# A first batch centred by an estimate of its mean and repaired afterwards, and a bias moved from ScalarE into VectorE's sum

## The chip, the cores and the metric

The kernel runs on one core of one Trainium2 chip. TensorE is called PE in the profile, VectorE DVE, ScalarE ACT, GpSimd POOL and SyncE SP. The metric is the device time of one execution in microseconds (us), and what counts is the median of several. The profile is of one further execution; its span runs from that execution's first to its last instruction.

## The reference

The input is x, 4 images of 48 channels and 256 x 256 pixels in float32. Four layers follow each other, each of the form x = x + layer(groupnorm(x)), the group norm having 16 groups of 3 channels without weights.

```python
def _L0_conv_ref(x, qkv_w, dw_w, proj_w, temperature):
    qkv = conv1x1(x, qkv_w)                      # 48 -> 144 channels
    qkv = depthwise3x3(qkv, dw_w)                # padding 1
    q, k, v = split(qkv, 3)                      # each 48 x 65536 per image
    q, k = l2_normalize(q), l2_normalize(k)      # along the pixels
    attn = softmax(q @ k.T * temperature)        # 48 x 48 per image
    return conv1x1(attn @ v, proj_w)

def _L1_conv_ref(x, W1, b1, gamma, beta, dw_w, dw_b, pw_w, pw_b, W2, b2):
    t = gelu(gelu(tokens(x) @ W1 + b1))          # 16 features
    x1, x2 = halves(t)
    n = layernorm(x2, gamma, beta)               # image of 8 channels
    g = x1 * ((depthwise3x3(n) + dw_b) * (conv1x1(n) + pw_b))
    return g @ W2 + b2
```

Layers 2 and 3 are recurrences over rows and columns (a five-tap convolution over channels, added line by line, down, up, right and left). The change doesn't touch them.

## The kernel before

**Layer 0, the sums over pixels (`layers01`, lines 122 to 624).** The attention matrix of an image needs only the products of q and k summed over all pixels, and these follow from "lag sums" of the input: for each shift of up to two pixels the 48 x 48 sums of x at a pixel times x at the shifted pixel. The input x has its group mean taken off first, so that a pixel outside the image counts as zero. For each image b (a batch here) nine pairs of pixel rows are loaded (`load_pair`, line 334; `raw`, 1728 KB each, four buffers), centred in place (`center`, line 341; three instructions a pair, with the means of `means_of`, line 307, which are spread to the rows by six matmuls into `pmask`) and turned into sums and differences (`points`, line 350; six DVE instructions, tiles `moving` and `still`, two buffers each). There are 16 units of work in a batch, two for each of eight pairs of neighbouring row pairs; unit u is 96 matmul calls (192 instructions) into three PSUM tiles `acc` (`sums`, line 367). After unit 15 the tiles are kept, combined to lags (`lags_of`, line 383) and turned into weights of the layer's convolution (`attention`, line 422); this runs in small pieces (`late`) between the next batch's matmuls.

**The statistics.** The mean of batch b + 1 is found while batch b is summed: 16 tiles of 96 x 2048 (`input_stats`, line 182, two loads of 384 KB a tile; called "I tiles" here), the first read by four `bn_stats` of DVE, the rest by two passes of ACT (`rough`, line 155, one writing a scrap tile `seen`, one in place). For batch 0 this stands ahead of the loop: lines 243 to 250 load 12 tiles of 128 x 2048 (`first_stats`, 1024 KB each, "F tiles"), four `bn_stats` each, and `first_norm` makes the mean and the coefficients of batch 0. Only then come the constants and the tap weights (lines 253 to 283), and the loop at line 590. All tiles of statistics share the pool `sums_p` with two buffers; of the F tiles before, every other one borrows a buffer of `moving`.

**Layer 0's convolution and layer 1.** From about 850 us the convolution runs block by block (`block`, line 679; a block makes 16 rows of one image, tile `y`, PSUM `py`). Of its 64 blocks those of image 0 run alone, the others between the pieces of layer 1 (`gated_layer`, line 781; `tick`, line 1067). A tick takes one of 32 strips through: tokens transposed (`ptok`), two projections with gelu (`ph`), a layer norm (`pm`, `pvar`, a reciprocal), convolutions (`psp`, `pch`), gate `g`, and with two ticks' delay the output: matmuls into `pout`, to which DVE adds the strip of x, `xr` (line 1027, 16 instructions of 96 x 256 a tick), after ACT has added the bias b2 to `xr` in place (`add_b2`, line 997, two passes of 96 x 2048 a tick). POOL then rearranges the result (`yr`, line 1034). While convolution blocks remain, `conv` pieces stand between the pieces of a tick; the last ticks have none left (`alone`).

**What sets the order.** Each engine and each DMA queue runs its instructions in the order of the built program. The framework that builds it decides that order from the order of the calls, its tiles and its own estimates; `tc.keep_in_program_order` pins single instructions. The order in the changed program, where the prediction speaks of it, was read from the built program. SP issues nearly all loads and stores, one after the other; an entry that waits for a buffer holds up all that follow.

Of the kernel before, what the change touches and what calls it, by code (L numbers as in the profile page):

```python
# [18 lines left out]
P = 96  # L19
# [102 lines left out]
def layers01(ctx, tc, x, xp, xe, inside, pick, rows, xc, x1, wqk, dwqk, wv, dwv, projT, temp, k, coef, coef1, gated, spare):  # L122
# [30 lines left out]
    seen = work.tile([P, n_st], F32, tag="seen", name="seen", bufs=1)  # L153

    def rough(b, i, t):
# [10 lines left out]
        for s, func in enumerate((AF.Identity, AF.Square)):  # L166
            kept = t if s else seen
            nc.scalar.activation(kept, t, func, bias=away, accum_out=sums[:, s, i - 1 : i])
# [28 lines left out]
    rows_sb = wp.tile([128, KR * (P + 128)], F32, tag="rows", name="rows_sb")  # L197
    nc.scalar.dma_start(rows_sb, rows)
    to_group = lambda m: rows_sb[:, P * m : P * m + P]
    to_row = lambda m: rows_sb[:P, KR * P + 128 * m : KR * P + 128 * m + 128]  # L200
    stat0 = work.tile([128, KR, 4 * NS, 6], F32, tag="st0_0", name="st0_0", bufs=1)
    x0 = x[0:C].rearrange("c (e n) -> (c e) n", e=8)

    def first_stats(i):
        m, part = divmod(i, NS)
        if i % 2:
            t = sums_p.tile([128, n_st], F32, tag="sx", name="sx")
        else:
            t = patch.tile([128, NPT * (PW // 2 + 4) * C], F32, tag="moving", name="sx")[:, :n_st]
        nc.sync.dma_start(t, x0[128 * m : 128 * m + 128, part * n_st : part * n_st + n_st])  # L210

        def add():
            for c in range(4):
                nc.vector.bn_stats(stat0[:, m, part * 4 + c, :], t[:, c * 512 : (c + 1) * 512])

        return add

    def first_norm():

        mv = work.tile([128, KR, 2], F32, tag="mv00", name="mv00", bufs=1)  # L220
        for m in range(KR):
            nc.vector.bn_aggr(mv[:, m], stat0[:, m].rearrange("p a b -> p (a b)"))

        def average(src, name):
            ps = p_small.tile([P, 1], F32, tag="small", name=name)
            for m in range(KR):
                nc.tensor.matmul(ps, lhsT=to_group(m), rhs=src(m), start=m == 0, stop=m == KR - 1)
            return ps

        nc.vector.tensor_copy(mean[0], average(lambda m: mv[:, m, 0:1], "pg"))  # L230
        ps = p_small.tile([128, KR], F32, tag="small", name="prows")
        for m in range(KR):
            nc.tensor.matmul(ps[:, m : m + 1], lhsT=to_row(m), rhs=mean[0], start=True, stop=True)
        d = work.tile([128, KR], F32, tag="d00", name="d00", bufs=1)
        nc.vector.tensor_sub(d, mv[:, :, 0], ps)
        nc.vector.tensor_mul(d, d, d)
        nc.vector.tensor_add(d, d, mv[:, :, 1])
        s = work.tile([P, 1], F32, tag="s00", name="s00", bufs=1)
        nc.scalar.activation(s, average(lambda m: d[:, m : m + 1], "pv"), AF.Sqrt, bias=k.eps[:P])
        nc.vector.reciprocal(coef[0][:, 0:1], s)  # L240
        nc.vector.scalar_tensor_tensor(coef[0][:, 1:2], mean[0], -1.0, coef[0][:, 0:1], ALU.mult, ALU.mult)

    waiting = []
    for i in range(KR * NS):
        waiting.append(first_stats(i))
        if len(waiting) > 3:
            waiting.pop(0)()
    for add in waiting:
        add()
    first_norm()  # L250


    wqk_sb = wp.tile([P, P], F32, tag="wqk", name="wqk_sb")
    nc.sync.dma_start(wqk_sb, wqk)
    wd = wp.tile([P, 3, 3, P], F32, tag="wd", name="wd")
    nc.gpsimd.dma_start(wd.rearrange("p x y o -> p (x y o)"), dwqk.rearrange("t o -> (t o)").partition_broadcast(P))
    for t in range(9):
        nc.vector.tensor_mul(wd[:, t // 3, t % 3, :], wd[:, t // 3, t % 3, :], wqk_sb)

    inside_sb = wp.tile([C, 6 * 128], F32, tag="inside", name="inside_sb")  # L260
    nc.sync.dma_start(inside_sb, inside)
    pick_sb = wp.tile([128, 3, 3, C], F32, tag="pick", name="pick_sb")
    nc.sync.dma_start(pick_sb.rearrange("p d k c -> p (d k c)"), pick)

    w0 = wp.tile([P, 3, 3, P], F32, tag="w0", name="w0")
    w1 = wp.tile([P, 3, 3, P], F32, tag="w1", name="w1")

    wc = wp.tile([P, 2, 2, P], F32, tag="wc", name="wc")
    for i in range(3):
        nc.vector.tensor_scalar_mul(w0[:, i], wd[:, i], half[:, 0:1])  # L270
        nc.vector.tensor_scalar_mul(w1[:, i], wd[:, i], half[:, 1:2])
    for side, tx in enumerate((2, 0)):
        nc.vector.tensor_add(wc[:, side, 0], w0[:, tx, 1], w1[:, tx, 2])
        nc.vector.tensor_add(wc[:, side, 1], w0[:, tx, 0], w1[:, tx, 1])

    wv_sb = wp.tile([C, 2 * 128], F32, tag="wv", name="wv_sb")
    nc.sync.dma_start(wv_sb, wv)
    dwv_sb = wp.tile([C, 9], F32, tag="dwv", name="dwv_sb")
    nc.sync.dma_start(dwv_sb, dwv)
    proj_sb = wp.tile([C, C], F32, tag="proj", name="proj_sb")  # L280
    nc.sync.dma_start(proj_sb, projT)
    temp_sb = wp.tile([C, 1], F32, tag="temp", name="temp_sb")
    nc.gpsimd.dma_start(temp_sb, temp.partition_broadcast(C))


# [21 lines left out]
    def means_of(b):  # L307

        dm = work.tile([C, C], F32, tag="dm", name="dm")
        nc.vector.tensor_scalar(dm, k["ident", C][:, :C], mean[b][:C], -1.0, ALU.mult, ALU.mult)  # L310
# [23 lines left out]
    def load_pair():  # L334

        b, r = pairs[len(raws)]
        t = patch.tile([128, 2, HALO * C], F32, tag="raw", name="raw", bufs=AHEAD + 1)
        nc.sync.dma_start(t, rows_of(xp[b], PH + 2)[:, 2 * r : 2 * r + 2])
        raws.append(t)

    def center(b, r, means):
# [3 lines left out]
        for i, w0, w1 in ((0, 1, PW // 2 + 1), (1, 0, 1), (2, PW // 2 + 1, HALO // 2)):  # L345
            here = wide[:, :, w0:w1]
            mean = means[:, v + i : v + i + 1].unsqueeze(1).to_broadcast([128, 2, w1 - w0, 2 * C])
            nc.vector.tensor_add(here, here, mean)

    def points(b, q, half):  # L350
# [6 lines left out]
        nc.vector.tensor_sub(bt[:, 0], d[0], d[2])  # L357
        nc.vector.tensor_add(bt[:, 1], d[1], d[2])
        nc.vector.tensor_add(at[:, 0], r[0], r[1])
        nc.vector.tensor_sub(bt[:, 2], d[2], d[1])  # L360
        nc.vector.tensor_sub(at[:, 1], r[0], r[1])  # L361
        nc.vector.tensor_sub(bt[:, 3], d[1], d[3])
# [20 lines left out]
    def lags_of(acc):  # L383
# [14 lines left out]
        def combined(d):  # L398
            ways = ((0, 0), (1, 0), (2, 0), (2, 1))
            out = held["out"] = p_small.tile([C, 5, C], F32, tag="small", name="plag")  # L400
            for n, (k, at) in enumerate(ways):
# [5 lines left out]
                    stop=n == len(ways) - 1,  # L407
# [177 lines left out]
    load_pair()  # L585
    load_pair()
    means[0] = means_of(0)
    for r in range(2):
        center(0, r, means[0])
    for g in range(B * NU + 1):  # L590
        b, u = divmod(g, NU)
        if g < B * NU:
            q, part = divmod(u, 2)
            if u == 0:
                of_batch[b] = (weights_of(b), *edges_of(b))
            if part == 0:
                while len(raws) < min(len(pairs), b * (N2 + 1) + q + AHEAD + 1):
                    load_pair()
                if q + 2 <= N2:
                    center(b, q + 2, means[b])  # L600
            new = points(b, q, part)
            if u == NU - 1 and b + 1 < B:
                means[b + 1] = means_of(b + 1)
# [7 lines left out]
        if g > 0:  # L611
# [6 lines left out]
            if u == NU - 1:  # L618
                while late:
                    some_late()  # L620
                first, lags = lags_of(acc)
# [159 lines left out]
def gated_layer(ctx, tc, banks, p_small, big, spare, x1, x2r, w1, w2, dw, ends, pw, cols, b2, k, coef1, coef2):  # L781
# [215 lines left out]
    def add_b2(c, ip):  # L997
        t = xrs[c, ip]
# [787 lines left out]
```

## Time and profile before

| | |
|---|---|
| median of 3 runs | 6943.6 us (6930.9 to 6946.0) |
| the profiled execution | 6936.42 us |
| its span | 6934.4 us |
| mean granted TensorE clock | 0.973 |
| busy: PE / DVE / ACT / POOL | 6569.4 / 3636.3 / 1844.0 / 2069.2 us |
| `acc` matmuls (L374), two forms | 685.6 and 682.5 us |
| sum of pout and xr (L1027) | 512 instructions, 176.7 us |
| bias of xr (L999) | 64 instructions, 127.5 us |
| statistics of batch 0 (L214) | 48 instructions, 28.9 us |

The page gives the busy time of each engine, the span in 40 slices (one is 173 us) with the busy share in tenths, the chain of work that ended last, and the costliest groups of instructions. A line of a timeline has the start in us, the time from the first to the last of a run of equal instructions, engine, line, operation, output <- inputs, shapes, the count, and in brackets the idle time before it with what ended it. A line of the waits has who waited for whom, the total in us, how many times and the longest. PE's busy time hides how fast it runs, and a wait on an engine that isn't the bottleneck costs nothing.

### The profile page before, as it was taken

The numbers are of one execution on the slowest core, as the hardware profiler recorded it, in microseconds if no ns is written. First come the engines' busy times: TensorE is split into PE (matmuls) and PEld (weight loads), VectorE is DVE, ScalarE is ACT, GpSimd is POOL, SyncE is SP. The second block draws the span as 40 slices with busy tenths as digits, with TensorE's granted clock in tenths as the row PEclk, the third lists the DMA queues.
The fourth block names the chain that finished last, engine by engine and source line by source line (L and its number), as shares of the span: only waits on it lengthen the run. The fifth ranks groups of instructions, "written<-read, shape, count | busy, mean of one in ns | idle before, by whom it ended". The sixth has DMA issues, their size and how long they took to land.

```text
span 6934.4 us, 133567 instructions
## 1 busy us (share of the span) xinstructions
PE 6569.4 (95%) x55772; PEld 5266.6 (76%) x55772; DVE 3636.3 (52%) x8740; ACT 1844.0 (27%) x2166; POOL 2069.2 (30%) x4211
## 2 busy tenths in 40 slices
PE   6999999999999779999998999986899999999999
PEld 4666633333333229999998999986899999999999
DVE  7777533555556554444444446754444444444444
ACT  3430022444444434444440000001544443000000
POOL 0000000233333554420004557652000000555777
PEclk9999999999999879999999999998999999999999
DMA  7742145677777769984669678989995566865775
GB/s 237 185 136 84 61 133 176 165 199 195 196 199 184 158 148 301 287 245 155 187 179 226 195 172 205 248 243 188 182 183 95 170 195 171 235 186 168 276 300 201
DMA packets 1177469, 1326.21 MB, mean 191 GB/s; under 512 B 831040, under 2 KB 1005760, under 8 KB 1124512
## 3 DMA queue, kind: packets, MB, share of 16 engines
q1 hardware_dynamic: 1163696, 1229.16, 65.4%
q10 hardware_dynamic: 13072, 88.18, 3.7%
q8 instruction: 437, 7.16, 0.4%
q14 instruction: 168, 1.38, 0.1%
q0 software_dynamic: 96, 0.33, 0.0%
HBM read 794.28 MB, written 522.19 MB: 190 GB/s over the span
## 4 chain that ended last, share of the span: by engine, by line
PE 86%; DVE 4%; DMA 3%; SPq 2%; ACT 2%; POOL 1%; issue 1%; ACTq 0%; POOLq 0%; DVEq 0%
PE ps L1227 57%; PE py L701 9%; PE acc L374 8%; PE py L710 5%; SPq L1263 2%; PE ph L830 2%; PE pout L1018 1%; PE psp L975 1%; DMA D<-d 1%; ACT d L1302 1%; POOL s L1512 1%; PE ptok L890 1%; DVE y L724 0%; DVE st L726 0%; DVE y L1027 0%
## 5 line engine op out<-in xcount | busy, mean ns | idle before, releaser
L1227 PE MATMUL ps<-d,w 128*128 128x128 f32 (+1 forms) x18360 | 2073.8, 276 | 104.3 <-DVE d L1233 61.1
L1227 PEld LDWEIGHTS ps<-d,w 128*128 128x128 f32 x18360 | 2069.2, 193 | 108.8 <-DVE d L1233 64.7
L1227 PE MATMUL ps<-r,w 128*128 128x128 f32 (+1 forms) x18360 | 2066.7, 276 | 68.7 <-POOL r L1444 36.0
L1227 PEld LDWEIGHTS ps<-r,w 128*128 128x128 f32 x18360 | 2064.6, 193 | 70.9 <-POOL r L1444 37.0
L1233 DVE SCALAR_TENSOR_TENSOR d<-ps,b,d 128x128 f32<-128x128 f32 x3054 | 979.7, 348 | 1155.4 <-PE ps L1227 1077.2
L1512 POOL TENSOR_TENSOR s<-s,r 128x128 f32<-128x128 f32 x1536 | 745.4, 521 | 334.3 <-DVE r L1233 331.0
L1233 DVE SCALAR_TENSOR_TENSOR r<-ps,b,pre 128x128 f32<-128x128 f32 x1530 | 490.3, 348 | 577.1 <-PE ps L1227 569.0
L1233 DVE SCALAR_TENSOR_TENSOR r<-ps,b,r 128x128 f32<-128x128 f32 x1530 | 490.1, 348 | 459.1 <-PE ps L1227 431.4
L374 PE MATMUL acc<-moving,raw 128*32 128x240 f32 (+1 forms) x6144 | 685.6, 381 | 12.3 <-DVE moving L357 11.5
L1444 POOL COPY pre<-c 128x128 f32<-128x128 f32 x1530 | 558.4, 404 | 464.3 <-DVE r L1233 462.5
L701 PE MATMUL py<-x1n,wy 128*96 128x512 f32 x1536 | 691.6, 599 | 0.0
L374 PE MATMUL acc<-moving,still 128*32 128x240 f32 (+1 forms) x6144 | 682.5, 381 | 6.8 <-DVE still L361 2.7
L1302 ACT ACTIVATE d<-x,spread 128x256 f32<-128x256 f32 x752 | 510.9, 824 | 550.2 <-DMA D<-d 380.6
L1383 ACT COPY u<-d 128x384 f32<-128x384 f32 x510 | 448.5, 900 | 573.5 <-DVE d L1233 541.0
L374 PEld LDWEIGHTS acc<-moving,raw 128*32 128x32 f32 x6144 | 430.0, 110 | 213.6 <-DVE moving L357 11.8
L701 PEld LDWEIGHTS py<-x1n,wy 128*96 128x96 f32 x1536 | 242.0, 163 | 410.8 <-issue 376.3
L1444 POOL COPY r<-c 128x128 f32<-128x128 f32 x6 | 2.4, 393 | 1691.2 <-DMA c<-U 1691.2
L724 DVE TENSOR_TENSOR y<-py,t 96x512 f32<-96x512 f32 x256 | 173.6, 678 | 462.1 <-PE py L710 462.0
L374 PEld LDWEIGHTS acc<-moving,still 128*32 128x32 f32 x6144 | 345.0, 110 | 34.7 <-issue 4.6
L710 PE MATMUL py<-x2n,wy 64*96 64x512 f32 x1536 | 360.8, 601 | 0.0
L1034 POOL COPY yr<-y 96x256 f32<-96x256 f32 x512 | 307.2, 648 | 129.4 <-DVE y L1027 128.4
L654 ACT ACTIVATE x1n<-t,g 128x2048 f32<-128x2048 f32 x64 | 134.2, 2096 | 696.1 <-PE py L701 573.9
(219 smaller groups left out, 4076.2 us busy)
## 6 DMA issues: line engine op xcount, KB each, us to landing
t<-in_xc SPq DMA_DIRECT2D x64, 1536.0 KB
c<-U SPq DMA_DIRECT2D x348, 256.0 KB
D<-d SPq DMA_DIRECT2D x54, 1536.0 KB
d<-D SPq DMA_DIRECT2D x54, 1536.0 KB
R<-r SPq DMA_DIRECT2D x54, 1536.0 KB
r<-R ACTq DMA_DIRECT2D x54, 1536.0 KB
U<-u SPq DMA_DIRECT2D x84, 768.0 KB
raw<-in_xp SPq DMA_DIRECT2D x36, 1728.0 KB
```

What stands on the lines that cost most here:

```text
L374: nc.tensor.matmul(out[32 * i : 32 * i + 32, : n * C], lhsT=still[i][:, first : first + 32], rhs=moving[:, i, lo : lo + n * C], start=u == ...
L701: nc.tensor.matmul(ps, lhsT=held["w"][0][:, dx], rhs=x1n[:, 2 * c : 2 * c + 2, dx : dx + W], start=dx == 0, stop=False)
L710: nc.tensor.matmul(held["ps"][q + 2 * s], lhsT=held["w"][1][here, dx], rhs=x2n[here, 2 * q : 2 * q + 2, dx : dx + W], start=False, stop=dx ...
L724: nc.vector.tensor_add(part, held["ps"][c], t1[:P, 2 * c : 2 * c + 2, :])
L830: nc.tensor.matmul(out[32 * q : 32 * q + 32], lhsT=w1_sb[:, half, i, :], rhs=moving(t), start=i < 4, stop=i >= 4)
L1034: made = nc.gpsimd.tensor_copy(yrs[c][:, :, 2 * i2 + ip, :].rearrange("p j (n a g) -> p j n a g", a=4, g=4)[:, :, :, al], y[:, i2, al].rea ...
L1227: nc.tensor.matmul(ps[m][:, here], lhsT=w[:, n, :], rhs=old[:, q, there], start=first, stop=last)
L1233: nc.vector.scalar_tensor_tensor(new[:, m], ps[m], bias[:, m : m + 1], inp[:, m], ALU.add, ALU.add)
L1302: pin(nc.scalar.activation(dst, src, AF.Identity, bias=g[:, 1:2], scale=g[:, 0:1]))
L1383: nc.scalar.copy(v[:, :, i, :, al], line)
L1444: nc.gpsimd.tensor_copy(dst[:, m].rearrange("p (J a b) -> p J a b", J=NBK, b=B), v[:, m, j, :, gl].rearrange("p J b a -> p J a b"),)
L1512: nc.gpsimd.tensor_add(v, v, line[:, m].rearrange("p (J a b) -> p J a b", J=NBK, b=B))
```

## The change

**Part 1.** Batch 0 is centred by an estimate of its mean, made ahead of its statistics. The host lays out the image's frame, the outer two pixels on every side (2032 pixels), as `xf` (128 x 768). `guessed` sums it and divides by 2048. The pixel pairs of batch 0 are centred with this estimate; the first two pairs are loaded and centred in two parts, the first halves of both ahead of the rest. The F tiles are now read during batch 0, one in most units, all from the pool `sums_p`; `first_norm`, cut into pieces, runs at the end of batch 0. As the estimate is off by a constant per channel, the lag sums of batch 0 get a repair: sums over the pixels that a shift moves out of the image (they all lie in the frame, `poff`: 20 matmuls), and one more matmul for each of three lag rows (`fixl`, `fixr`). These terms are sums over the true mean and the estimate, so that the lags come out as with the true mean. The weights and edges of batch 0 are made after its last unit. The constants move to ACT's and POOL's queues, behind the first halves; the taps are made after unit 2's points. On the way, DVE's instructions up to unit 2 are pinned, and `rough` drops the scrap tile: the second pass of ACT reads what the first wrote.

**Part 2.** `add_b2` goes; the bias is added in DVE's sum of `pout` and `xr`.

```diff
-        for s, func in enumerate((AF.Identity, AF.Square)):
-            kept = t if s else seen
-            nc.scalar.activation(kept, t, func, bias=away, accum_out=sums[:, s, i - 1 : i])
+        nc.scalar.activation(t, t, AF.Identity, bias=away, accum_out=sums[:, 0, i - 1 : i])
+        nc.scalar.activation(t, t, AF.Square, accum_out=sums[:, 1, i - 1 : i])
...
+    xf_sb = wp.tile([128, NF, C], F32, tag="xf", name="xf_sb")
+    nc.scalar.dma_start(xf_sb.rearrange("p k c -> p (k c)"), xf)
...
-        if i % 2:
-            t = sums_p.tile([128, n_st], F32, tag="sx", name="sx")
-        else:
-            t = patch.tile([128, NPT * (PW // 2 + 4) * C], F32, tag="moving", name="sx")[:, :n_st]
+        t = sums_p.tile([128, n_st], F32, tag="sx", name="sx")
...
+    def guessed():
+        part = work.tile([128, C], F32, tag="gpart", name="gpart", bufs=1)
+        nc.vector.reduce_sum(part, xf_sb.rearrange("p k c -> p c k"), axis=AX.X)
+        ps = p_small.tile([P, 1], F32, tag="small", name="pguess")
+        nc.tensor.matmul(ps[:C], lhsT=part, rhs=k["ones", 128][:, 0:1], start=True, stop=True)
+        nc.vector.tensor_scalar_mul(guess[:C], ps[:C], 1.0 / (128 * NF))
...
+        def outside():
+            ps = held["ps"] = p_small.tile([48, 2, C], F32, tag="small", name="poff")
+            for i in range(NF):
+                nc.tensor.matmul(ps[:, 0], lhsT=off(i), rhs=xf_sb[:, i], start=i == 0, stop=False)
+            for i in range(3):
+                nc.tensor.matmul(ps[:, 0], lhsT=fixed(i), rhs=dg[:, i], start=False, stop=i == 2)
+            nc.tensor.matmul(ps[:, 1], lhsT=k["ones", C][:, :48], rhs=dg[:, 2], start=True, stop=True)
+
+        def factors():
...
+            nc.vector.tensor_mul(
+                right, at.unsqueeze(1).to_broadcast([48, NL, C]), which.unsqueeze(2).to_broadcast([48, NL, C])
+            )
...
-    waiting = []
-    for i in range(KR * NS):
-        waiting.append(first_stats(i))
-        if len(waiting) > 3:
-            waiting.pop(0)()
-    for add in waiting:
-        add()
-    first_norm()
...
+            if b == 0:
+                nc.tensor.matmul(
+                    out.rearrange("p l c -> p (l c)"),
+                    lhsT=fix["left"],
+                    rhs=fix["right"][:, 5 * d : 5 * d + 5].rearrange("p l c -> p (l c)"),
+                    start=False,
+                    stop=True,
                 )
...
-    load_pair()
-    load_pair()
-    means[0] = means_of(0)
+    load_pair(None, 0, FIRST)
+    load_pair(None, 0, FIRST)
+    load_part(0, FIRST, HALO * C, raws[1][:1, 1, FIRST - 1 : FIRST])
+    load_part(1, FIRST, HALO * C)
+    for _ in range(2):
+        load_pair(raws[1][:1, 1, HALO * C - 1 : HALO * C])
+    load_fixed(raws[1][:1, 1, FIRST - 1 : FIRST])
+    guessed()
+    means[0] = means_of(guess)
     for r in range(2):
-        center(0, r, means[0])
+        center(0, r, means[0], 0)
+    firsts = list(range(KR * NS))
...
-                if q + 2 <= N2:
+                if g > 0 and q + 2 <= N2:
                     center(b, q + 2, means[b])
+            if g == 1:
+                for r in range(2):
+                    center(0, r, means[0], 1)
             new = points(b, q, part)
+            if g == 1:
+                center(0, 2, means[0])
+            if g == 2:
+                make_taps()
+                early.clear()
+            if b == 0:
+                for n in range(len(firsts) - KR * NS * max(fed - 1 - u, 0) // fed):
+                    while len(adding) > 1:
+                        adding.pop(0)()
+                    adding.append(first_stats(firsts.pop(0)))
+                if u == fed:
+                    while adding:
+                        adding.pop(0)()
+                    for piece in first_norm():
+                        late.append(piece)
...
-                first, lags = lags_of(acc)
+                if b == 0:
+                    of_batch[0] = (weights_of(0), *edges_of(0))
+                first, lags = lags_of(b, acc)
...
-    def add_b2(c, ip):
-        t = xrs[c, ip]
-        nc.scalar.activation(t, t, AF.Identity, bias=b2_sb)
-
...
-                nc.vector.tensor_add(y[:, q % 2, 2 * kk + q // 2, :], ps[q][:, kk], t[:, 4 * kk + q, :])
+                nc.vector.scalar_tensor_tensor(
+                    y[:, q % 2, 2 * kk + q // 2, :], ps[q][:, kk], b2_sb, t[:, 4 * kk + q, :], ALU.add, ALU.add
+                )
...
-            pieces += [conv] + turned(0, 1) + of_now(centered) + turned(3) + of_old(gate) + added
+            pieces += [conv] + turned(0, 1) + of_now(centered) + turned(3) + of_old(gate)
```

The one-element copies of POOL in `load_part` and `load_fixed` write into the tile that is loaded next, reading the end of one that must have landed; the load then waits for them, which sets the order of the loads.

## The prediction

> **What bounds the kernel now.** I read the page first: the slices of its second part and the chain of its fourth.
>
> ```profile
> span 6934.4 us, 133567 instructions
> PE   6999999999999779999998999986899999999999
> ...
> PE 86%; DVE 4%; DMA 3%; SPq 2%; ACT 2%; POOL 1%; issue 1%; ACTq 0%; POOLq 0%; DVEq 0%
> ```
>
> PE is the bound nearly everywhere. Two places stand out: the first slice (6) and slices 14 and 15 (77). The change touches just these two, so everything between counts only if it breaks PE's cover.
>
> Then the timeline of the first 72 us, for the first place.
>
> ```profile
> 11.44 9.80 DVE L214 BATCH_NORM_STATS2 st<-sx 128x6 f32<-128x512 f32 x16 [11.44 <-DMA sx<-in_x]
> ...
> 49.85 2.76 PE L313 MATMUL pmask<-dm,inside_sb 48*128 48x48 f32 x12 [3.52 <-ACT ends L304]
> ...
> 53.57 3.90 DVE L348 TENSOR_TENSOR raw<-raw,means 128x3072 f32<-128x3072 f32 x3
> ...
> 64.13 1.01 PE L374 MATMUL acc<-moving,raw 128*32 128x240 f32 x2 [11.52 <-DVE moving L357]
> ...
> 71.01 1.15 DVE L357 TENSOR_TENSOR moving<-raw 128x960 f32<-128x960 f32 x1
> ```
>
> The reader sees 48 statistics instructions (16 in 9.8 us, so 2.45 us a tile of four), then the norm, the centring, and only at 64.13 the first product; the points of unit 0 are complete at 71.1. From there PE sets the pace: the loads of raw pairs, each waiting for PE, are issued at 92.08, 112.80, 133.52, 154.24 and 174.96, so two units take 20.72 and one 10.36 us. Batch 0 ends at 245.4, where ACT's copy of acc stops waiting.
>
> For the second place I read the waits between 2240 and 2640 us, where the last images run without convolutions between them.
>
> ```profile
> DVE y L1027 <- ACT xr L999: 23.5, 7, 5.8
> ```
>
> Seven times DVE's sum waited for ACT's bias. The timelines of ACT and DVE show one turn:
>
> ```profile
> 2424.93 1.29 ACT L946 ACTIVATE n<-d,col 128x512 f32<-128x512 f32 x1 [4.22 <-DVE d L944]
> 2426.02 1.96 ACT L999 ACTIVATE xr<-xr,b_sb 96x2048 f32<-96x2048 f32 x1
> ```
> ```profile
> 2428.01 2.74 DVE L1027 TENSOR_TENSOR y<-pout,xr 96x256 f32<-96x256 f32 x8 [3.11 <-ACT xr L999]
> ```
>
> PE's next matmul (ph, 2428.91) waits for that y.
>
> **Part 1, the start.** Removed ahead of the first product: twelve F tiles (first batch's statistics, 1 MB each), the norm and the taps. Put there: xf, 0.39 MB, at the place in ACT's queue where rows_sb (0.34 MB) was, whose last packet ended at 5.2 us in the trace; I take 6.2. Then the sum over 768 elements 0.9 (a 768-column still takes 0.95), its matmul and copy 0.8, dm 0.25, the pmask row 2.8, three copies 1.06: means at 12.1. The two first halves land in the place of the first F tiles (first read at 11.44). Centring them is 1920 of 3456 columns of a 3.81 us pitch each, 4.3 together: 16.4. First moving: **17.5**; points take 6.02 a unit (243.53 to 249.54 in DVE's timeline), so unit 0's are complete at 22.4. That is 48.7 us earlier. The sum over xf reads with a stride and has no row of its own, no more than the repair's broadcast product later (48x720): I take the plain rows of their size (0.95, and 0.8 for 720 columns), and as the dear end 3.35, the reciprocal of 512 columns, the slowest DVE row of that size. Bounds of the first product: 17 (centring right at 11.44) and 24 (xf served only with the second F tile, whose last packet ended at 12.9).
>
> **What takes its place in batch 0.** The rest of the loads moves behind the first halves: the second halves, the fixed tensors (1.5 MB, now on ACT's and POOL's queues) and raws 2 and 3 are 5.8 MB, from 13.8 to 28.6 at 390 GB/s (380 was the rate of 40 to 60 us), so F0 is there at 32. POOL's one-element copies order them: 0.1 us like its memsets, up to 0.65 like its smallest copies; nothing waits for them, as centre 2 begins at 31.9.
>
> DVE per two units: 12.0 points, 3.8 centring, 1.71 F tiles at 2.45: 20.0 of PE's 20.72. It fits, but with no room, and the order on DVE is fixed: in the changed program it runs points 0, rest of the centring, points 1, centre 2, F0, I0 (I: next batch's tiles), F1, centre 3, points 2, taps and F2, points 3. Step by step: points 1 end 31.9, centre 2 35.7, F0 and I0 with their few small sums 41.0. F1 may be loaded only when F0's buffer is read (38.2); 1 MB takes 2.5 us (419 GB/s in the DMA view while F tiles came alone), start and landing 2.1: DVE idles to 42.8. Then F1 45.3, centre 3 49.1, points 2 55.1. PE, which began unit 1 at 33 (a unit ends some 10.6 us after its points when PE was idle), is done with it at 43.3 and gets unit 2 only now: **11 us lost**. Taps (4.9) and F2 make points 3 end at 68.5, unit 3 three late; by unit 6 the sum of losses is 16, and the one turn where a centring and an F tile stand inside the points (unit 10) adds 1.5. From then PE is the bound. 22.4 + 10.6 + 15 x 10.36 + 17.5: batch 0 ends at **206**, for 245.4.
>
> The loads: raw, I and F tiles need 4.4 to 4.9, 3.45 and 2.5 us of the DMA engines, 17.1 per 20.72 us, so they fit. SP's queue is in order, and the tiles alternate between two buffers, so nearly all I tiles follow each other in one. A turn of it is landing plus two passes of ACT (4.2):
>
> ```profile
> 92.08 0.35 SPq L338 DMA_DIRECT2D raw<-in_xp  x1
> 92.54 16.85 SPq L186 DMA_DIRECT2D sx<-in_x  x6
> ```
> ```profile
> 104.36 2.00 ACT L168 ACTIVATE seen<-sx,away 96x2048 f32<-96x2048 f32 x1 [6.87 <-DMA sx<-in_x]
> ```
>
> Behind a raw the turn is 11.8 + 4.2 = 16.0; alone it was 9.9 (free at 108.5, landed 114.4). Stepping through SP's order gives the last I tile done at 198, 12.1 a turn over 13 turns from 41. PE asks for it at 81% of unit 15, about 203: it is hidden, by 5 to 8 us.
>
> **The turn of the batches.** Before, the next batch's norm stood in unit 14, and its two pairs were centred (7.7 us) beside unit 15. In the changed program the norm's matmuls come at 81% and 89% of unit 15, then those of batch 0's own norm, and pmask only after all of batch 0. DVE has its points 15 done but nothing to centre with. From 206: the two norms' interlocked small steps 3.8, pmask 2.8, copies 1.1, two centrings 7.6, copies for the repair 0.7, centre 2 and the repair's factors 4.7 (they stand ahead of the points), points 6.0: unit 0 of batch 1 is ready at **233**, before 249.5. So 16.5 us stay of 39: 23 are given back. The 20 matmuls of poff (0.24 us a pass, 9 us) lie beside the centrings; if DVE outran them they would cost 1. Unknown here are the small steps; none (all hidden) to twice my 3.8.
>
> A rule weighed against this: before, the first products after an idle PE took 0.61 us (at 65.2), later ones of the same shape 0.366. The changed kernel lets PE idle twice more, some 7 us and 20 us. [...] The rows I use are of products after idling too, so I add nothing.
>
> **Part 2, the bias.** Removed: 64 ACT passes of 1.99 us. Changed: 512 sums, tensor + tensor into scalar_tensor_tensor. With 512 columns the row of L926 (two tensors) has 674 ns and L982 (with a column) 751, so 0.07 us more each, 37 in all. In the ticks from 1250 to 2250 us DVE is busy 27 to 32 of 50 us and PE 49.8: both cost and relief are hidden there; without that cover it is +37. In the ticks without convolutions a turn of 31.1 us loses the 3.1 us wait: the sum then follows DVE's d directly (2424.9 for 2428.0), its pout was done at 2424.7, POOL is free from 2423.7. Next late are ACT's queue entries for near (until 2429.0), after which ph is read as before, so PE runs ahead and the turn closes over PE's row, 3.1 shorter. Of 23.5 us I take off ten turns x 0.3 for the slower sums that gate PE and POOL, and 2 for the one 5.8 us wait behind which a DMA stood: **18**. Bounds: 24 gained; or 5 lost (no wait saved, 0.07 on the 60 sums of the chain).
>
> The in-place passes on sx change nothing on the path: ACT is idle a third of that time. If each waited 0.2 us for the one ahead, a turn of the I tiles would be as much longer, and 198 would be 201.
>
> **Sum.** 6936.4 of the profiled execution (span 6934.4 and 2.0 around it) - 16.5 - 18 = 6902. The median shown is 7 above that execution (6943.6; 6930.9 to 6946.0); with half of that: **6905**.
>
> **Rivals.**
> 1. The turn of the batches hides, since DVE may find its means earlier than I step them: another 15 to 20 us, 6885. For it: small steps of 0.15 us each. Against: pmask stands behind batch 0 on PE.
> 2. The sums' wait is replaced in the last ticks by near's DMA or POOL's copies (POOL yr stands in the chain with PE): only the start counts, 6922.
> 3. The loads starve DVE: its statistics stand in line with its points, so an F tile that is late stops both. At 2.5 us for each of the twelve 30 us go, 6935, no difference that can be told. For it: DVE at 97% of PE's pace. Against: in my stepping every tile from F2 on lands 2 us or more ahead of its use, but for F6, which comes just in time.
> 4. Slower, by one mechanism: the buffer of the I tiles. Its 13 turns end at 198 with 12.1 each. From 12.7 on, every microsecond of the mean turn delays PE at unit 15 by 13. At 15.3 all 34.5 us are gone; at 16.4 the kernel is 0.2% slower, about 6957. For it: 16.0 was measured whenever a raw stood ahead, and F tiles now stand there as well. Against: two of three turns were 9.9 to 12.
>
> **Chances.** Forecast 0.54; rival 1 0.11; rival 2 0.09; rival 3 0.14; rival 4 0.12. A measurement of this kernel tells 0.2% (14 us) from no change. Forecast, 1 and 2 are faster by more than that: 0.74; rival 3 is within: 0.14; rival 4 slower: 0.12. The range leaves out rival 4 and the far end of 1: 6878 to 6940.
>
> **What would show it.** Right: the first acc matmul near 17.5; PE waiting for DVE's moving between 43 and 55 and again for some 20 us after 206; no other gap; DVE's y at 0.48 us and never waiting for ACT; the ticks without convolutions 18 us shorter than before. Wrong: a wait of PE's pg for the last sx (rival 4); DVE waiting on sx all along batch 0 (rival 3); y waiting for DMA or yr in the last ticks (rival 2); or a longer stretch from 1250 to 2250, which would mean that DVE's slower sums lost PE's cover.

## The result, and the profile after

The changed kernel took 6883.3 us in the median of four runs (6875.7 to 6899.0), the kernel before 6938.5 beside it: a ratio of 0.9923 (95% interval 0.9911 to 0.9935). Five more runs, beside other runs of the kernel before, gave 6891.8 against 6934.0, 0.9937 (0.9925 to 0.9950). It is 44 to 53 us faster, where 6905 (6878 to 6940) was predicted. The total lies inside the range, 13 to 22 us under the value; its two parts were not right. Part 1 brought 12 us in place of 16.5, Part 2 37 in place of 18.

The page of the changed kernel, its first, second and fourth part:

```profile
span 6897.2 us, 133551 instructions
PE   8999999999999869999989999985999998999999
PE 87%; DVE 5%; DMA 3%; SPq 2%; POOL 1%; ACT 1%; issue 1%; ACTq 0%; POOLq 0%; DVEq 0%
```

The first slice has gone from 6 to 8. Slices 14 and 15 read 86 for 77: here the page is too coarse, since a stretch that gets shorter hands the rest of its slice to what follows. The marks below show it.

The start, in PE's and DVE's timelines of the changed kernel:

```profile
18.02 1.81 PE L450 MATMUL acc<-moving,raw 128*32 128x240 f32 x4 [7.20 <-DVE moving L433]
```
```profile
36.47 2.47 DVE L218 BATCH_NORM_STATS2 st<-sx 128x6 f32<-128x512 f32 x4
38.86 2.45 DVE L189 BATCH_NORM_STATS2 st<-sx 96x6 f32<-96x512 f32 x4
45.57 2.48 DVE L218 BATCH_NORM_STATS2 st<-sx 128x6 f32<-128x512 f32 x4 [3.78 <-DMA sx<-in_x]
56.69 1.15 DVE L438 TENSOR_TENSOR moving<-raw 128x960 f32<-128x960 f32 x1
```

The first product comes at 18.0 (64.1 before). Then DVE reads F0 and I0 and stands idle for F1, whose load had to wait for F0's buffer; the points of unit 2 are only ready at 57.8.

The turn of the batches, in DVE's timeline:

```profile
208.16 0.18 DVE L170 TENSOR_REDUCE tot<-sums 96x2 f32<-96x30 f32 x1 [14.49 <-ACT sx L166]
...
221.86 0.46 DVE L374 COPY means<-pmask 128x288 f32<-128x288 f32 x1 [2.34 <-PE pmask L372]
...
222.78 7.70 DVE L424 TENSOR_TENSOR raw<-raw,means 128x3072 f32<-128x3072 f32 x6
...
235.89 1.14 DVE L433 TENSOR_TENSOR moving<-raw 128x960 f32<-128x960 f32 x1
```

And PE's waits from 0 to 260 us (total, times, longest):

```profile
PE acc L450 <- DVE moving L433: 16.9, 3, 9.1
...
PE pg L94 <- DVE tot L175: 2.4, 1, 2.4
```

DVE waits until 208 for the last I tile, PE with it for 2.4 us; the chain of small steps and pmask takes until 221.9, and batch 1's first points are ready at 241.9 (249.5 before). Of PE's three waits for points one stands ahead of the first product (7.2), the longest ahead of unit 2 (9.1, at 53.0) and 0.6 at the turn, where PE waits for the repair's copies instead (4.9, `fixt`).

For Part 2, the group of the sum over the whole span:

```profile
L1134 DVE SCALAR_TENSOR_TENSOR y<-pout,b_sb,xr 96x256 f32<-96x256 f32 x512 | 205.9, 471 | 13.4 <-PE pout L1125 13.4
```

It never waits for ACT, and one sum costs 0.062 us more than the 0.409 of before.

This profiled execution (6899.0) is the slowest of its four, and one reason stands in the windows: the granted clock (the first number behind POOL's) fell while PE was busy throughout. The second fence is PE's timeline just ahead of the dip (`pgram` is a step of `attention`).

```profile
500.00:520.00 20.00, 20.00 (x282) 13.32 (x278) 14.71 (x17) 0.00 (x0) 0.53 (x1) 1.00 0.14 57
520.00:540.00 20.00, 20.00 (x272) 15.73 (x268) 11.57 (x14) 0.00 (x0) 0.31 (x1) 0.84 0.25 91
```
```profile
530.25 0.41 PE L577 MATMUL pgram<-wdg,pj 48*96 48x96 f32 x2
```

Three such dips up to 960 us cost about 8 us (the last section returns to them). So a second execution of the same kernel was profiled (called the second profile below, span 6880.7), without them. Where the time went is read from marks in these traces (us; a mark is the start of the row that it names):

| mark | before | Part 1 alone | Part 2 alone | both, 2nd profile | both, 1st |
|---|---|---|---|---|---|
| last acc of batch 0 kept | 247.0 | 213.5 | 247.8 | 213.6 | 218.7 |
| last acc of batch 3 kept | 849.1 | 838.6 | 848.6 | 834.8 | 847.8 |
| first ph (layer 1 begins) | 1205.9 | 1195.4 | 1205.4 | 1191.6 | 1206.3 |
| last py (convolutions end) | 2247.5 | 2239.8 | 2240.7 | 2227.2 | 2242.2 |
| first ps (recurrences begin) | 2604.4 | 2592.0 | 2558.3 | 2542.2 | 2560.6 |
| span | 6934.4 | 6921.4 | 6895.9 | 6880.7 | 6897.2 |

### The profile page after: what moved, and what is told of

The parts are those of the page before. It is cut to its first block, busy times and chain, and to the rows that moved or that the text cites. A ratio compares the mean times of both kernels' runs of the same rounds, so it can differ in the third digit from the quotient of the medians.

```text
span 6897.2 us, 133551 instructions
## 1 busy us (share of the span) xinstructions
PE 6573.2 (95%) x55826; PEld 5283.3 (77%) x55826; DVE 3668.5 (53%) x8754; ACT 1728.3 (25%) x2103; POOL 2075.3 (30%) x4219
## 4 chain that ended last, share of the span: by engine, by line
PE 87%; DVE 5%; DMA 3%; SPq 2%; POOL 1%; ACT 1%; issue 1%; ACTq 0%; POOLq 0%; DVEq 0%
PE ps L1335 58%; PE py L812 9%; PE acc L450 7%; PE py L821 5%; PE ph L941 2%; SPq L1371 2%; PE pout L1125 1%; PE psp L1086 1%; DMA sx<-in_x 1%; DMA D<-d 1%; DVE y L1134 1%; ACT d L1410 1%; POOL s L1620 1%; DVE raw L424 1%; DVE st L837 0%
## 5 line engine op out<-in xcount | busy, mean ns | idle before, releaser
L1335 PE MATMUL ps<-d,w 128*128 128x128 f32 (+1 forms) x18360 | 2073.8, 276 | 107.8 <-DVE d L1341 64.3
```

The costliest lines, as they stand in the source:

```text
L1335: nc.tensor.matmul(ps[m][:, here], lhsT=w[:, n, :], rhs=old[:, q, there], start=first, stop=last)
```

## The experiments

Theory A came from the two traces: Part 1 keeps little, Part 2 carries the change, for more than its visible wait. Theory B was the split of the forecast. Each set of experiments had its own runs of the kernel before beside it (medians 6934 to 6941); "under" and "over" are in us against those, or against the changed kernel where that is said.

**Part 1 alone.**

```diff
+        nc.scalar.activation(t, t, AF.Identity, bias=b2_sb)      # add_b2, as before
-                nc.vector.scalar_tensor_tensor(y..., ps[q][:, kk], b2_sb, t[:, 4 * kk + q, :], ALU.add, ALU.add)
+                nc.vector.tensor_add(y..., ps[q][:, kk], t[:, 4 * kk + q, :])
```

> The changed kernel with ACT's bias passes and the plain sum put back: Part 1 alone. Theory A (read from the two traces: Part 1 gains 46 us at the start, gives back nearly all by the end of layer 0, and the alone ticks carry the change): 5 to 10 us under the kernel before, about 6930, with the last I tile done near 208 us and the alone ticks (2250 to 2604 in the kernel before) as long as before, 355 us. Theory B (the split of the forecast): 16 under, about 6922; then the rest of the 55 us that the medians differ by comes from both parts together. In the changed kernel's profile the granted clock fell to 0.84 to 0.97 with PE fully busy at 520 to 540, 720 to 760 and in 900 to 1000 us, about 8 us in all. If Part 1 makes it, it is there again at the same places; if it belongs to that one execution, it is not.

6927.6, 0.9983 (0.9974 to 0.9992): 12 us under, 6 to 18. That lies between A and B and excludes neither; the marks give 10 us at the end of layer 0 and 12 at the first ps. The three dips of the clock are not there, but one is, at 325 us.

**Part 2 alone**, the reverse edit on the kernel before.

> The kernel before with the bias moved into DVE's sum: Part 2 alone. Theory A: 40 to 47 us under the kernel before, about 6895, and the alone ticks 316 us in place of 355. Theory B: 18 under, about 6920, alone ticks 337. Both expect no change from 1250 to 2240 us.

6907.5, 0.9947 (0.9935 to 0.9960): 37 under, 28 to 45, and with Part 1's 12 this makes 49, as both together do. B's 18 is excluded. The ticks alone took 317.6 (A: 316), but the convolution's ticks, where both expected nothing, also lost 6 us (1041.6 to 1035.4 between first ph and last py), and from the first ps to the end 8 us were given back (4330.0 to 4337.6). So the ticks hold 39 + 6, and 37 are left.

Why 39, when the sum had waited 23.5? The trace answers it. One turn of the ticks alone was 31.1 us before and 23.3 after: 7.8 less, of which the sum's wait is 3.1. The turns in PE's timeline, before and (second fence) in the second profile:

```profile
2397.79 1.89 PE L830 MATMUL ph<-xt,w_sb 128*32 128x512 f32 x2 [4.55 <-DVE y L1027]
...
2428.91 1.88 PE L830 MATMUL ph<-xt,w_sb 128*32 128x512 f32 x2 [4.20 <-DVE y L1027]
```
```profile
2380.86 1.06 PE L941 MATMUL ph<-xt,w_sb 128*32 128x512 f32 x6 [1.11 <-DVE y L1134]
...
2404.20 1.06 PE L941 MATMUL ph<-xt,w_sb 128*32 128x512 f32 x6 [1.11 <-DVE y L1134]
```

In windows of the kernel before (PE's busy time first, then PEld, DVE, ACT, POOL, then the granted clock):

```profile
2424.00:2429.00 5.00, 0.80 (x9) 0.12 (x2) 1.78 (x5) 3.05 (x2) 0.51 (x1) 0.81 0.78 170
2429.00:2432.00 3.00, 3.00 (x4) 0.45 (x4) 3.00 (x9) 2.97 (x4) 2.31 (x5) 0.50 1.10 219
2432.00:2435.00 3.00, 3.00 (x10) 0.59 (x10) 1.13 (x2) 1.74 (x2) 1.99 (x4) 0.50 0.30 60
2435.00:2438.00 3.00, 3.00 (x8) 0.20 (x6) 0.00 (x0) 0.00 (x0) 0.00 (x0) 0.50 1.06 226
```

and of the second profile of the changed kernel:

```profile
2404.00:2407.00 3.00, 2.80 (x16) 0.69 (x17) 3.00 (x9) 0.65 (x1) 2.08 (x4) 1.00 1.03 228
2407.00:2410.00 3.00, 2.94 (x14) 0.99 (x10) 2.02 (x5) 2.57 (x4) 2.46 (x5) 1.00 0.16 24
```

Both begin with the same 16 ph and 4 pout; before, they ran at half the clock. The ph that follow the wait, grouped, first before and then after (last column: PE's idle time just ahead):

```profile
L830 PE MATMUL ph<-xt,w_sb 128*32 128x512 f32 x16 | 5.7, 1060 | 4.2 <-DVE y L1027 4.2
```
```profile
L941 PE MATMUL ph<-xt,w_sb 128*32 128x512 f32 x16 | 3.0, 601 | 1.1 <-DVE y L1134 1.1
```

Before, PE stood idle for 4.2 us because ph waits for y, which frees a tile of the pool `banks` (line 629); the clock fell to 0.50 and 16 ph and 4 pout took 9.44 us (2428.91 to 2438.35). After, PE waits 1.1 us, the clock stays at 1.00, and they take 4.87 (2404.20 to 2409.07). That is 4.6 us a turn on top of the 3.1: 7.7 of the 7.8. Six turns of the kernel before had this wait.

The windows over all of the ticks alone (last py to first ps) say the same of the whole stretch. PE has the same matmuls in each (923 or 924 are in the records), and a longer busy time goes with a lower clock:

| ticks alone | us | PE busy | PE idle | granted clock |
|---|---|---|---|---|
| before | 356.9 | 259.9 | 97.0 | 0.78 |
| Part 2 alone | 317.6 | 239.3 | 78.3 | 0.82 |
| both, 2nd profile | 315.0 | 232.1 | 82.9 | 0.85 |
| both, 1st profile | 318.4 | 239.4 | 79.0 | 0.82 |
| ACT occupied (next) | 331.6 | 254.3 | 77.3 | 0.78 |

Of Part 2's 39 us, 18.7 are idle time of PE and 20.6 its clock.

**ACT as occupied as before, but nobody waits for it.**

```diff
+        for i in range(5):
+            nc.scalar.activation(scrap, t[64:96, i], AF.Identity, bias=b2_sb[64:96])
```

> The changed kernel, but ACT still reads each xr, in five passes of 32x256 into a scrap row that nobody reads (about 2 us, as the bias pass took), so ACT is as occupied as before while the sums wait for nobody but PE. If the wait of the sum on ACT was the whole price (theory A1, the step of the forecast): within 5 us of the changed kernel's 6883. If it was ACT's time in its queue (A2: the passes stand ahead of the entries for gate and norm, 2 x 2 us a turn): 20 to 45 above it, with alone ticks of 335 to 355 us. In between, both count.

6913.1, 0.9962 (0.9950 to 0.9975): by the ratios 17 to 27 over the changed kernel, where A1 had at most 5 and A2 20 to 45. Part 2 brings 37, so 10 to 20 are left for the sum's wait: both count. PE's ph again waits 1.1 us and one turn is again 23.3 (2406.0 to 2429.3). But the ticks alone take 331.6 for the 315 to 318 of the changed kernel, and the ticks with convolutions 1047.1 for 1035.6. There lies the second cause, ACT's time: the passes stand between those for h in its queue, where the chain of the ticks alone runs through them, and the norm at an image's end waits again. By the table the price in the ticks alone is the clock once more: PE idles no longer than in the changed kernel, but its matmuls take 15 to 22 us more. Which of ACT's passes brings which dip was not found. PE's waits from 1210 to 2235 us in this kernel, and below in the kernel before:

```profile
PE pv L102 <- DVE gn_d L98: 8.9, 4, 3.7
```
```profile
PE pv L102 <- DVE gn_d L98: 6.5, 4, 2.6
```

In Part 2 alone this wait is 2.3. Here too the clock adds to the wait: in the kernel before, from the end of the longest of the four (2.57 us) on, it was 0.50 from 1874.1 to 1880.9, with PE busy for 6.3 us; with ACT occupied it was so twice (1480.3 to 1487.2, 1869.5 to 1876.3), in Part 2 alone and in both profiles of the changed kernel never. So the 6 us of the ticks with convolutions are some 4 of waiting and, by an estimate from these rows, 3 at half clock. The five short passes took 160.8 us of ACT where the bias had taken 127.5, so the experiment prices ACT's time a quarter too high.

**No bias at all.**

```diff
-                nc.vector.scalar_tensor_tensor(y..., ps[q][:, kk], b2_sb, t[:, 4 * kk + q, :], ALU.add, ALU.add)
+                nc.vector.tensor_add(y..., ps[q][:, kk], t[:, 4 * kk + q, :])
```

> The changed kernel with the plain sum of two tensors and no bias at all (it leaves out the bias b2, which is zero in this input): the price of the slower sum, 0.062 us x 512 = 32 us of DVE. Forecast's step: hidden in the ticks with convolutions, 0.3 us a turn in the ten alone, so 3 us under the changed kernel. If all 16 sums of an alone turn stand on the path: 10 under. If the cover in the other ticks is gone: up to 32 under.

6876.7, 0.9905 (0.9890 to 0.9920), 7 and 15 under the changed kernel's two medians. Inconclusive: the four runs fell at 6869 and 6884, and the changed kernel itself at 0.9923 and 0.9937. By the marks it spends 1035.8 and 314.7 in the two kinds of ticks, as the second profile of the changed kernel does (1035.6 and 315.0). By these marks the dearer sum costs little, as forecast; how little was not resolved.

**A third buffer for the tiles of statistics.**

```diff
-    sums_p = sctx.enter_context(tc.tile_pool(name="a_sums", bufs=2))
+    sums_p = sctx.enter_context(tc.tile_pool(name="a_sums", bufs=3))
```

The room comes from xf and edge sharing a tile, and from one buffer in place of two for wdg and cols, which are therefore made in unit 12 of batches 1 to 3 and not in unit 0.

> The changed kernel with a third buffer for the tiles of statistics (the room comes from xf and edge sharing a tile, and from single buffers for wdg and cols, which are therefore made in unit 12 of batches 1 to 3). Theory: F1 no longer waits for F0's buffer, so DVE doesn't idle ahead of it (3.8 us in the changed kernel) and points 2 end near 54; the last I tile is done at 198 to 204 in place of 206 to 208; PE's pg waits for nothing. 5 to 8 us under the changed kernel, about 6876. Rival: the order on DVE and SP sets these times and not the buffer, so the last I tile stays at 206 or later: within 3 us of it.

6875.4, 0.9912 (0.9898 to 0.9925); run again beside the changed kernel:

> The kernel with the third buffer once more, on the same chip as the changed kernel. Its trace has batch 0's turn and all that follows 18 to 20 us earlier than the changed kernel's cleaner traces; the medians of two calls differ by 8 only. If the trace is right: 12 to 20 us under the changed kernel of this call. If something gives half of it back in most executions: 5 to 9 under.

6872.6, 0.9911 (0.9896 to 0.9926), 19 under the changed kernel's 6891.8 beside it. The theory was right and too timid: F1 follows at once (DVE starts it at 42.0, no idle time), the wait for pg is gone, and the last I tile is done here:

```profile
188.93 0.17 DVE L170 TENSOR_REDUCE tot<-sums 96x2 f32<-96x30 f32 x1
```

17 to 20 us earlier than with two buffers, the points of batch 1 are ready at 218.6, and the last acc of layer 0 is kept at 818.7, 16 us ahead of the changed kernel's second profile and 20 ahead of Part 1 alone.

**Batch 0's norm moved into batch 1.** Its pieces and the repair's factors run behind batch 0's copy of acc; batch 1's weights and edges are made in unit 6.

```diff
-                    for piece in first_norm():
-                        late.append(piece)
...
+                    for piece in first[:1] + norm[:n_w] + [make_of] + norm[n_w:] + first[7:]:
+                        late.extend([piece, lambda: None])
```

> The changed kernel with batch 0's own norm and the repair's factors moved out of the turn of the batches: they run as pieces in batch 1, behind the copy of acc; the weights and edges of batch 1 are made in its unit 6. PE then goes from the next batch's norm to pmask at once. Theory: points of batch 1's first unit are ready near 229 in place of 237 to 242; poff's 20 matmuls, which lay beside the centring, now cost PE 5 to 9 us in batch 1, so only 0 to 5 us under the changed kernel remain, about 6880. Rival: the turn is set by the last I tile and the centrings alone: points not earlier, and the time 5 to 9 over it.

6890.3, 0.9939 (0.9927 to 0.9952): no gain that can be told. The points of batch 1 came at 231.4 in place of 236.2 (second profile), but PE kept batch 1's last acc at 436.7 as there: what the turn gained was lost in batch 1, where the repair's matmuls now stand, while PE idles for 11.8 us in the turn that they had filled. The profiled execution (6905.9, the slowest of its five) also shows what one trace can hold: its ticks alone took 328.5 us, with PE busy for 248.9, though their code is the changed kernel's.

> Both of the above in one kernel: third buffer and batch 0's norm in batch 1. If the two costs add: last I tile near 200, points of batch 1's first unit ready near 222, 8 to 14 us under the changed kernel, about 6872. If the late tile hides the small steps (one cost, not two): as the better of the two alone.

6869.1, 0.9904 (0.9889 to 0.9919): 14 and 23 under the changed kernel's two medians, and with the third buffer alone (0.9911, 0.9912) the best version of those that compute all. The points came at 212.1; whether the second edit adds to the first can't be told apart.

**No F tiles.** The loads and statistics of batch 0 are left out, and its coefficients with them.

```diff
-    firsts = list(range(KR * NS))
+    firsts = []
+    nc.gpsimd.memset(stat0, 1.0)
```

> The changed kernel without the twelve F tiles: it leaves out the loads and statistics of batch 0 (its coefficients come out wrong), and measures what they cost in batch 0. Theory (the forecast's steps): no idle DVE at unit 2, the 16 us lost by unit 6 fall to 3 or less, I tiles have both buffers; batch 0 ends near 195, and the turn gives the rest: 12 to 20 us under the changed kernel, about 6867. Rival: the loss at unit 2 comes from DVE's own work (rest of the centring, points 1, centre 2 and 3 and the taps, one after the other), so only 5 us go.

6858.9, 0.9888 (0.9874 to 0.9901): 24 to 33 under the changed kernel, more than expected. The points of unit 2 are ready at 51.3, those of batch 1 at 211.4. The last acc of layer 0 is kept at 811.4, for 818.7 with a third buffer and 834.8 in the second profile: of the 23 us that the F tiles cost there, the buffers they share are some 16. Whether the other 7 are DVE's time (2.45 us a tile), their loads or something else, no run separates.

**The changed kernel once more.**

> The changed kernel once more, beside the others of this call. Its first execution with a profile lost about 8 us to dips of the granted clock with PE fully busy (520 to 960 us), which no other kernel's profile showed. If those belong to that execution: the clock is 1.00 there, layer 0's last acc is kept near 838 in place of 848, and the time is 6880 to 6890.

6891.8; the profiled execution, 6882.5, has no dip of the clock from 260 to 1000 us and the last acc at 834.8. The dips belong to single executions.

**F tiles from unit 2 on**, two buffers.

```diff
-                for n in range(len(firsts) - KR * NS * max(fed - 1 - u, 0) // fed):
+                for n in range(len(firsts) - KR * NS * max(fed - 1 - u, 0) // (fed - 2)):
```

> The changed kernel with the F tiles read in units 2 to 13 in place of 0 to 13, two buffers as in the changed kernel. Theory (the buffer of the I tiles decides the end of batch 0): DVE no longer idles for F1 at unit 2 and PE gets unit 2 some 5 us earlier, but the last I tile still ends at 204 or later, so at most 3 us under the changed kernel. Rival (the loss at unit 2 decides): 5 to 8 under.

6898.5, 0.9947 (0.9934 to 0.9959): no gain, so the rival was wrong, and the theory had the right buffer but expected no loss. The median is 7 us over the changed kernel's beside it, with intervals that overlap; the last acc of layer 0 is kept at 849.9, 15 later than in the second profile, of which two dips of the clock make some 3. The start did as meant: the points of unit 2 were ready at 51.4 in place of 57.8. But twelve F tiles in twelve units push the I tiles further back, the last is done at 215.2, and PE's waits show the price:

```profile
PE pg L94 <- DVE tot L175: 11.5, 1, 11.5
PE acc L450 <- DVE moving L433: 9.3, 3, 7.2
```

This is the mechanism of the forecast's rival 4, whole: PE earlier, the last I tile later, 11.5 us of waiting for it.

**All three edits.**

> Third buffer, batch 0's norm in batch 1, and F tiles from unit 2 on, in one kernel. The kernel with the first two was at 6869 (0.9904 of the kernel before) and still lost 7 us at unit 2 and 5 in the turn; with the F tiles out of unit 1 I expect 3 to 6 us less, about 0.990. If DVE has too little room later in the batch for twelve F tiles in twelve units: no gain over it.

6879.9 (6867 to 6891), 0.9920 (0.9905 to 0.9935): no gain over the first two, as the second alternative had it.

## Why the prediction was right in its range and wrong in its parts

**First product 17.5, points of unit 0 at 22.4:** 18.0 and 22.8. Right.

**Unit 2.** DVE idle to 42.8, points 2 at 55.1, points 3 at 68.5; measured 45.6, 57.8 and 70.0. The step is right, its load is mis-sized: F1 was issued at 38.97 (38.2 by my steps), but DVE could begin with it only 6.6 us later, not 4.6 (2.5 for the transfer and 2.1 for start and landing, of which the 2.1 were my estimate, with no row of their own). Probably this is because loads of an I tile (41.34) and a raw pair (43.90) were issued beside it, where I had taken the rate of F tiles alone. Two sums in my account of the loads are a little off: the loads of two units come to 16.1 us by their own terms (4.9, two I tiles, 1.71 F tiles), not 17.1, and the turn of an I tile alone to 10.1, not 9.9.

**Last I tile at 198, and rival 4.** Measured 206.4 to 208.7 in six traces with these tiles and buffers: a mean turn of 12.7 to 12.9 us over 13 turns from 41, where I had 12.1. The threshold of rival 4 was 12.7, and 13 us per microsecond beyond it; at 12.86 (208.2) this gives 2.1, and PE's pg waited 2.4 there, 1.6 and less in the others. So the kernel sits on the threshold of the rival to which I gave 0.12. The in-place passes had no part in it: two passes take 4.13 us (59.92 to 64.05 in ACT's timeline), as before (104.36 to 108.49).

**Turn of the batches.** The first centring, at 213.7 by my steps, began at 217.1 in the second profile. In the first it was 222.8: there the last I tile came 1.7 us later, and after PE's wait for pg, at a low clock (0.74 from 200 to 220 us), the same small steps took 4 us more. From there on all went as worked out: 13.1 us to the points (7.6 + 0.7 + 4.7) and 6.0 for them. Ready at 236.2 (241.9 in the first profile) for 233. So Part 1 kept 13 us of the 16.5 there, and 12 (6 to 18) in the time. Of the 48 that unit 0 had gained, the F tiles cost 24 to 33, by the experiment without them.

**The rule weighed against Part 1.** In the kernel before, the first products after an idle PE took 0.61 us in place of 0.37; I added nothing for the new gaps. What that left out was not measured by itself: in the first profile the granted clock fell to 0.74 (40 to 60 us) and 0.59 (220 to 240 us), with PE busy for 10.8 and 12.7 of each 20 us and DVE for 16.2 and 18.0. The place where the clock decided was Part 2, and there I did not look at it.

**Part 2: 18.** This is the step that failed: "PE runs ahead and the turn closes over PE's row, 3.1 shorter". It took the wait of DVE's sum for the price. Behind it stood PE's own wait of 4.2 us for that y, in the profile of before for every such turn, and ph at 1.06 us behind it; the same form in the same trace at full clock takes 0.60. With 16 ph and 4 pout at half rate a turn is 7.7 shorter, not 3.1. The 6 us in the ticks with convolutions, from ACT's queue, were forecast as nothing. That part of the gain is given back in the recurrences I did not foresee: from the first ps to the end they took 4330 us before and with Part 1 alone, 4338 with Part 2 alone, and 4333 to 4344 in the eleven other profiles. The cause is open: the waits of ps for d grew by some 3 us in the first profile (61.1 to 64.3), but not in the second (61.2).

**Rivals.** 1, 2 and 3 as such didn't come: y never waits for near's DMA, POOL's yr waits less for y (82 us for 128), and DVE waited for F tiles for 5.8 us in all, 3.8 of them F1. That the total fell into the range is partly luck: Part 1 was 4 us too much and Part 2 19 too little, and the range, made for other reasons, was wide enough for the difference.

## What to carry to other kernels

Price a wait by what runs behind it: where PE idles for about 4 us in every turn, look at the granted clock in the windows right after it and at the mean time of the same matmul elsewhere; removing the wait gave back both here (3.1 and 4.6 us a turn). Work moved under cover of another stage took buffers there as well as engine time (some 16 of the F tiles' 23 us), so count the turns of every shared buffer, and if a stepped value comes within a few per cent of a threshold, give the rival more than 0.12. One execution's trace can hold 8 us or more of its own, so compare marks over several before a cause is named.

## What the runs showed of the hardware

- The half clock outlasted the wait. With an idle time of 4.2 us (2424.7 to 2428.9) the kernel before was granted 0.50 from 2427.1 to 2440.7, 13.6 us, with PE busy for 11.8 of them; the rows give 4.6 us for the ph and pout alone. With one of 1.1 us (2403.1 to 2404.2, second profile) the clock stayed at 1.00. But dips came with waits between the two as well: 2.57 us in the kernel before (1872.0 to 1874.6, clock 0.50 from 1874.1), and in the second profile 1.5 and 1.8 us within 6 us, ahead of 0.50 from 2422.6 to 2429.4.
- The clock also fell to 0.50 with PE busy throughout, mostly behind small matmuls. Six of the eight dips found between 260 and 1000 us in the fourteen profiles began 3.3 to 3.6 us after the first pgram: 18 matmuls of 48x96, one every 0.17 us (first profile: pgram at 530.25, clock 0.50 from 533.8 to 540.6; Part 1 alone: 321.88, and 325.4 to 332.3). A seventh began behind 18 matmuls of 48x288 (`ptap`, first profile, 957.0), the eighth, the only one with PE idle, behind a wait of 1.9 us. Five lasted 6.8 us, which loses 3.4 each; three lasted 3.4. The other 50 times that pgram stands in these profiles the clock stayed at 1.00 behind it, so small matmuls alone don't decide it; the dips are one source of the spread between runs (about 8 us between 260 and 1000 us in the first profile, none there in the second).
- Adding a column in DVE's sum of a PSUM and an SBUF tile costs 0.062 us for 96x256 (0.409 to 0.471), and an ACT pass over 96x2048 that reads what the pass just ahead wrote in place costs no more than one whose input was there before (4.13 us for the two, both ways).
